# A graph layer with scattered messages: slots found earlier, shorter last segments, two banks for sums, a smaller first tile

## The chip, the cores and the metric

The kernel runs on one core of one Trainium2 chip. Its time is device microseconds of one execution; the median of three executions is given beside the time of one further execution that the hardware profiler recorded. A core has TensorE (PE, matmuls, with weight loads shown apart as PEld), VectorE (DVE), ScalarE (ACT), GpSimd (POOL) and SyncE (SP). SP, ACT and POOL can issue transfers (DMA), which share 16 DMA engines.

## The reference

One layer of message passing over 12,500 nodes of 128 features and 412,500 edges sorted by `dst`, then a residual. `ssp` is softplus minus log 2, and `idx_i` is `src`, `idx_j` is `dst`.

```python
h = jnp.maximum(_layernorm(x, axis=-1), 0.0)
h = h @ W_in2f
Wij = ssp(f_ij @ W_f1 + b_f1) @ W_f2 + b_f2
Wij = Wij * rcut_ij[:, None]
x_ij = h[idx_j] * Wij
agg = jax.ops.segment_sum(x_ij, idx_i, num_segments=h.shape[0])
out = x + ssp(agg @ W_o1 + b_o1) @ W_o2 + b_o2
```

The gather runs along the sorted index, so the rows that 512 consecutive edges gather lie close together. The sum runs along the unsorted one.

## The kernel before, in words

**Chunks and groups.** Edges go in chunks of 512 (`CH`), four tiles of 128; four chunks are a group. There are 806 chunks in 202 groups. The program is written out with no loop on the chip, and the order on each engine is the order of the calls in `step(k)`, which works on message k and on later chunks at once.

**Per chunk.** `hidden`, `hidden_log` and `hidden_end` make the softplus of the edge features, two chunks at a time (PE, three ACT passes, one DVE operation). `value` multiplies by `W_f2` into a PSUM bank and adds the bias by one matmul of `ones_b` with `bf12_p`, which holds the bias as three bf16 parts. `rows` loads a window of 32 node rows from a table in HBM (`near`), at a row that SP reads from a list; `window` and `pick` select each edge's row by a one-hot matmul; `picked` scales by the edge weight (ACT). `message` multiplies the two (L800) into a buffer `o` that holds two chunks, of which there are four. POOL then scatters each tile of 128 messages, 129 numbers each (the last is the node's place in its block of 128), by one indirect DMA into a table of slots in HBM (L804).

**Slots.** A message's slot must be free and lie in the region of its node block (98 blocks). `blocks` compares block numbers (DVE, L689), `rank` runs two matmuls over a PSUM bank `free` that carries the counts, `rank_end` takes a maximum (DVE, L713) and every group turns the result into slot numbers. This runs up to six chunks ahead of the messages (`LR`).

**Segments.** The groups are cut into segments (`SEGS`), each with its own slot table, T tiles a block (one more where a segment's own nodes lie), cleared by SP beforehand. When all messages of a segment have been scattered, `Collect` sums them: a unit is up to 6 tiles (`UT`) loaded by SP (`m`, five buffers, L842), compared with 128 places by DVE (`to`, L853), and multiplied into one PSUM bank `acc` (PE, L866) that holds a quad of four blocks. After a quad `keep` adds the bank to `agg` (DVE, L889; ACT for the first segment). Units of all segments but the last are spread over the steps by a schedule with a constant rate between the segments' ends. The last segment is collected after all chunks, in 25 quads, and each quad goes through `finish`: loads of x, matmul with `W_o1`, softplus (four ACT passes), `r` addition (L435), `x + b_o2` (DVE, L438), matmul with `W_o2`, addition (L446), store.

**Start.** `make_h` makes the node rows for a quad of four tiles (statistics, normalisation, transposes, matmul, three bf16 parts) and stores them in every table of `tables` that has them. The first table holds the first 512 rows and serves chunks 0 to 8. Two quads are made beside the first chunks, the rest from `side()`, one every nine steps. Then `bias_parts` splits the bias by eight small DVE operations.

**Fallback.** The flags in `bad` are read at the end, and `anyway` recomputes the layer if one is set. No record of it is in the profile.

Of the kernel before, what the change touches and what calls it, by code (L numbers as in the profile page):

```python
# [9 lines left out]
F32 = mybir.dt.float32  # L10
# [12 lines left out]
SEGS = (88, 40, 30, 14, 14, 8, 8)  # L23
# [6 lines left out]
UT = 6  # L30
# [11 lines left out]
def gnn_kernel(  # L42
# [38 lines left out]
    class Segment:  # L81
# [4 lines left out]
        def __init__(self, k):  # L86
# [7 lines left out]
            mean = (SEGS[k] * TG * P - (own[1] - own[0])) / QT * P / N  # L94
# [32 lines left out]


    tables = [(0, QN)]
# [4 lines left out]
    for c in range(NC):  # L134
        n = c * CH * N // n_edges
        table_of.append(0 if n < QN - NEAR - P else min(n // QN, NQ - 1) + 1)
# [46 lines left out]
    def load_x(q):  # L183
        n = min(QT, NTILE - q * QT)
        full = min(n, N // P - q * QT)
        xb = ln.tile([P, QT, P], F32, name="xb")
        if full < n:
            nc.vector.memset(xb[:, full:n, :], 0.0)
            nc.sync.dma_start(xb[:N % P, full, :], x[q * QN + full * P:N, :])
        if full:  # L190
            nc.sync.dma_start(xb[:, :full, :], x[q * QN:q * QN + full * P, :]
                              .rearrange("(c p) f -> p c f", p=P))
        return xb
# [60 lines left out]
    def constants():  # L254
# [3 lines left out]
        first_load(0)  # L258
        nc.sync.dma_start(win, w_in2f)

        for j in range(NCHUNK):
            nc.sync.dma_start(wf1[32 * j:32 * j + RBF, :], w_f1)

        nc.scalar.preload_act_table_set("natural_log_exp_and_others")
        nc.scalar.dma_start(bf1, b_f1[:, None])
        nc.scalar.dma_start(wf2, w_f2)
        nc.scalar.dma_start(bf2, b_f2[None, :].to_broadcast([P, P]))
# [4 lines left out]
        prow_i = early_room[:WP, rows_at + 5 * NC:rows_at + 5 * NC + 1].bitcast(I32)  # L272
# [7 lines left out]
        nc.gpsimd.memset(ones_b, 1.0)  # L280
        nc.gpsimd.memset(bf12_p, 0.0)
# [9 lines left out]
        nc.vector.memset(bad, 0.0)  # L291
        nc.vector.memset(rel[:, NPART - 1, :], 0.0)
        nc.vector.memset(ones, 1.0)
        nc.vector.memset(none, 0.0)

        for t in range(QT):
            nc.vector.memset(turn[:, :, t:t + 1], -1.0 if t % 2 else 1.0)
        nc.vector.tensor_scalar(prow_i, prow_i, 7, None, op0=ALU.logical_shift_right)
        nc.vector.tensor_copy(prow, prow_i)
# [3 lines left out]

    def biases(psum):

        nc.vector.tensor_scalar(nbf1, bf1, -1.0, None, op0=ALU.mult)
        b12 = psum.tile([P, QT, P], F32, name="b12", tag="acc")[:, 0, :]
        nc.tensor.matmul(b12, bf1.to_broadcast([P, P]), wf2, start=True, stop=True)
        nc.vector.tensor_add(bf12, b12, bf2)

    def bias_parts():

        left = bf12[:3, :]
        for k in range(3):
            part = ln.tile([3, P], BF16, name="bias_part", bufs=1)
            nc.vector.tensor_copy(part, left)
            nc.vector.scalar_tensor_tensor(bf12_p[:3, :], part, ident[:3, k:k + 1],
                                           bf12_p[:3, :], op0=ALU.mult, op1=ALU.add)
            if k < 2:
                nc.vector.tensor_sub(left, left, part)  # L320

    def late_loads():
        nc.sync.dma_start(wo1, w_o1)
        nc.sync.dma_start(wo2, w_o2)
        nc.sync.dma_start(bo1, b_o1[:, None])
        nc.sync.dma_start(bo2, b_o2[None, :].to_broadcast([P, P]))

    early = {}
    quads = []


    def make_h(q, psum):

        n = min(QT, NTILE - q * QT)
        xb = early.pop(q, None)
        if xb is None:
            xb = load_x(q)
# [41 lines left out]
        for (b, rows), table in zip(tables, h3_t):  # L379
            lo = max(0, b - q * QN) // P  # L380
            hi = min(n, (b + rows - q * QN) // P)
            if lo < hi:
                r = q * QN + lo * P - b
# [3 lines left out]
                if b + rows == QN:  # L387
                    yield
            if q == NQ - 1:
# [4 lines left out]
            h3[q * QN:q * QN + n * P, :].rearrange("(c p) f -> p c f", p=P),  # L394
            hb[:, :n, :, :].rearrange("p c k f -> p c (k f)"))
        yield
# [15 lines left out]
    def finish(t0, n, sT, quad, psum, tag="v", bufs=3):  # L412
# [13 lines left out]
        yield  # L426

        z = psum.tile([P, 2, CH], F32, name="z_out", tag="z")[:, 0, :n * P]
# [7 lines left out]
        for p, cs, rows in pieces:  # L436
            xi = xo[:p, cs, :]
            nc.vector.tensor_add(xi, xi, spread(bo2[:p, :], xi.shape[1]))  # L438
# [94 lines left out]
    with tc.tile_pool(name="edge", bufs=2) as edge, tc.tile_pool(  # L533
# [46 lines left out]
        class Group:  # L580


            def __init__(self, g):
# [3 lines left out]
                if g % NB == 0:  # L587
                    f = edge.tile([P, NB, CH], F32, name="f")
                    for j in range(NCHUNK):
                        nc.sync.dma_start(f[32 * j:32 * j + RBF, :, :],  # L590
                                          f_t[g:g + NB, j].rearrange("b k n -> k b n"))
                    kept["f"] = f
                self.f = kept["f"][:, g % NB, :]
                i = g - self.seg.g0
                if i % SB == 0:
                    w = min(SB, ceil_div(self.seg.c1, NCHUNK) - g) * TG
                    cols = slice(g * TG, g * TG + w)
                    src_i = edge.tile([P, SB * TG], I32, name="src_i")
                    nc.sync.dma_start(src_i[:, :w], src_t[:, cols])
                    rcut = edge.tile([P, SB * TG], F32, name="rcut")  # L600
                    nc.sync.dma_start(rcut[:, :w], rcut_t[:, cols])
                    kept["cols"] = [w, src_i, rcut]
                self.cols = kept["cols"]
                self.at = slice(i % SB * TG, (i % SB + 1) * TG)
                if g == 0:
                    rel_store(0)
                self.rel = edge.tile([WP, NCHUNK, CH], BF16, name="rel", bufs=4)
                nc.sync.dma_start(self.rel, rel_d[g * NCHUNK:(g + 1) * NCHUNK, :][None, :, :]
                                  .to_broadcast([WP, NCHUNK, CH]))
                self.inb = {}  # L610
                self.pair = {}
                self.near = {}

            def rows(self, c):

                k = self.g * NCHUNK + c
                t = table_of[k]
                i = int(k >= FIRST)
                at = k - heads[i].start
                self.near[c] = edge.tile([WP, P], BF16, name="near", bufs=8)  # L620
                start = nc.sync.value_load(shifts[i][0:1, at:at + 1], min_val=0,
                                           max_val=tables[t][1] - WR)
                nc.sync.dma_start(self.near[c], h3_t[t][bass.ds(start, WR), :]
                                  .rearrange("r (k f) -> (r k) f", f=P))

            def columns(self):
                if len(self.cols) == 3:
                    w, src_i, _ = self.cols
# [7 lines left out]
                    place = edge.tile([P, SB * TG], F32, name="place")  # L636
                    nc.vector.tensor_copy(place[:, :w], src_i[:, :w])

# [22 lines left out]
                self.rcut, self.blk, self.place, self.start = (t[:, self.at] for t in self.cols[2:])  # L661

            def hidden(self, c):

# [576 lines left out]
```

## Time and profile before

| quantity | value |
|---|---|
| median of three executions | 5252.87 us (5247.94 to 5257.49) |
| the profiled execution's own time | 4236.61 us |
| its span, first to last instruction | 4234.9 us |
| mean granted TensorE clock in it | 0.882 |
| DMA, mean over the span | 194 GB/s |
| sum matmuls, L866 | 8132 |
| compares, L853 | 824 |
| additions to `agg` by DVE, L889 | 150 |
| scatters, L804 | 3224 |

The profiled execution is 1016 us shorter than the median. Durations below are its own. A row of a group gives the line, engine, operation, tile written and read and the count; then busy time in us and the mean ns of one; then the idle time of the engine just before, and what ended it. A wait row gives who waited for what, the total in us, the times and the longest.

### The profile page before, as it was taken

How to read it: one execution, taken by the hardware profiler on the slowest of the kernel's cores; microseconds unless marked ns; L12 is line 12 of the kernel's file. 1: busy time of each engine (PE TensorE's matmuls, PEld its weight loads, DVE VectorE, ACT ScalarE, POOL GpSimd, SP SyncE). 2: the span in 40 equal slices, each digit the busy share in tenths (PEclk: the TensorE clock that was granted, in tenths of full speed). 3: DMA queues.
4: the chain of work that ended last, by engine and by line, in shares of the span. 5: the costliest groups of instructions: out<-in, count | busy, mean ns of one | idle time of the engine just before them, and what ended most of it. 6: DMA issues, size and time to landing. Idle time of an engine off the chain costs nothing. (4 is left out here: it accounts for less than half of the span.)

```text
span 4234.9 us, 73728 instructions
## 1 busy us (share of the span) xinstructions
PE 3371.9 (80%) x22378; PEld 2543.6 (60%) x22378; DVE 3352.9 (79%) x6752; ACT 2329.8 (55%) x4686; POOL 3095.9 (73%) x3246
## 2 busy tenths in 40 slices
PE   6766666666666666689998899898898988888888
PEld 4444444444444444467777777777776777767777
DVE  8877766776666656678888888888888998999978
ACT  5665565655555555555555555555555555555535
POOL 5777777777777777777777777777777777777760
PEclk9877877877777777789999999999999999999999
DMA  5765555555444454366787777877787768767667
GB/s 171 213 192 180 176 175 177 157 159 159 126 118 132 121 164 125 107 193 210 229 269 213 216 212 211 267 229 218 214 243 234 229 203 270 234 203 204 184 183 232
DMA packets 515591, 820.92 MB, mean 194 GB/s; under 512 B 177075, under 2 KB 312871, under 8 KB 515187
## 3 DMA queue, kind: packets, MB, share of 16 engines
q1 hardware_dynamic: 411586, 602.85, 49.2%
q0 software_dynamic: 103168, 213.15, 15.3%
q8 instruction: 181, 2.97, 0.3%
q14 instruction: 224, 1.83, 0.1%
q10 hardware_dynamic: 432, 0.13, 0.0%
HBM read 419.09 MB, written 396.64 MB: 193 GB/s over the span
## 5 line engine op out<-in xcount | busy, mean ns | idle before, releaser
L804 POOL DMA_INDIRECT slots<-o,slot x3224 | 3092.5, 959 | 1010.8 <-issue 770.3
L769 PE MATMUL v<-wf,r 128*128 128x128 f32 x6448 | 1066.6, 317 | 540.7 <-DVE o L800 539.1
L769 PEld LDWEIGHTS v<-wf,r 128*128 128x128 f32 x6448 | 924.7, 221 | 590.3 <-DVE o L800 571.2
L789 ACT ACTIVATE hg<-picked,rcut 128x128 f32<-128x128 f32 x3224 | 907.7, 368 | 630.9 <-PE picked L780 292.5
L866 PEld LDWEIGHTS acc<-to,m 128*128 128x128 f32 x8132 | 1017.2, 201 | 235.9 <-issue 142.0
L866 PE MATMUL acc<-to,m 128*128 128x128 f32 x8132 | 1078.8, 289 | 32.5 <-DVE to L853 22.1
L675 ACT ACTIVATE a<-z,bf 128x1024 f32<-128x1024 f32 x403 | 450.4, 1118 | 853.5 <-PE z L668 853.0
L668 PE MATMUL z<-f,wf 20*128 20x512 f32 x1612 | 527.2, 734 | 224.8 <-DVE r L684 223.3
L853 DVE TENSOR_TENSOR to<-count_ps,m 128x512 f32<-128x512 f32 (+3 forms) x824 | 641.8, 804 | 65.6 <-DMA m<-slots 34.7
L800 DVE TENSOR_TENSOR o<-v,hg 128x512 f32<-128x512 f32 x806 | 550.5, 683 | 48.8 <-PE v L771 25.0
L798 DVE COPY o<-place 128x8 f32<-128x8 f32 x403 | 77.0, 191 | 610.6 <-DMA slots<-o,slot 609.9
L760 DVE TENSOR_TENSOR at<-count_ps,rel 96x512 bf16<-96x512 f32 x806 | 545.7, 677 | 0.0
L684 DVE SCALAR_TENSOR_TENSOR r<-z,nbf,a 128x1024 f32<-128x1024 f32 x403 | 513.9, 1275 | 21.1 <-ACT a L677 21.1
L677 ACT ACTIVATE a<-a,half 128x1024 f32<-128x1024 f32 x403 | 462.8, 1148 | 13.1
L713 DVE TENSOR_REDUCE top<-free 128x4 f32<-128x392 f32 x806 | 446.7, 554 | 8.1 <-PE free L708 8.1
L689 DVE TENSOR_TENSOR inb<-count_ps,blk 128x392 f16<-128x392 f32 x806 | 447.4, 556 | 0.0
L676 ACT ACTIVATE a<-a 128x1024 f32<-128x1024 f32 x403 | 426.0, 1057 | 12.8
L780 PEld LDWEIGHTS <-at 96*128 96x128 bf16 x3224 | 256.0, 105 | 251.1 <-DVE at L760 104.0
L668 PEld LDWEIGHTS z<-f,wf 20*128 20x128 f32 x1612 | 138.8, 210 | 409.6 <-DVE r L684 362.2
L780 PE MATMUL picked<-near,at 96*128 96x128 bf16 x3224 | 343.2, 234 | 32.1 <-DVE at L760 26.8
L771 PE MATMUL v<-bf_p,ones_b 128*128 128x512 bf16 x806 | 353.3, 438 | 0.0
L741 PE MATMUL free<-inb,rest_of 128*128 128x392 f16 x806 | 302.9, 376 | 12.6 <-DVE top L713 12.6
(112 smaller groups left out, 1428.2 us busy)
## 6 DMA issues: line engine op xcount, KB each, us to landing
m<-slots SPq DMA_DIRECT2D x311, 387.0 KB
m<-slots SPq DMA_DIRECT2D x317, 258.0 KB
rel<-rel_d SPq DMA_DIRECT2D x202, 384.0 KB
m<-slots SPq DMA_DIRECT2D x172, 322.5 KB
slots<-o,slot POOLq DMA_INDIRECT x3224
slots<-zero SPq DMA_DIRECT2D x96, 387.0 KB
slots<-zero SPq DMA_DIRECT2D x64, 516.0 KB
f<-in_f_t SPq DMA_DIRECT2D x404, 80.0 KB
```

The source lines that it names most:

```text
L668: nc.tensor.matmul(z[:, k, :], wf1[rows, :], self.f[rows, :], start=True, stop=True)
L675: nc.scalar.activation(a, z, AF.Abs, bias=bf1)
L677: nc.scalar.activation(a, a, AF.Ln, bias=half, scale=0.5)
L684: nc.vector.scalar_tensor_tensor(r, z, nbf1, a, op0=ALU.max, op1=ALU.add)
L760: nc.vector.tensor_tensor(at, prow_ps.to_broadcast([WP, CH]), self.rel[:, c, :], op=ALU.is_equal)
L769: nc.tensor.matmul(v[:, i, :], r[:, i * P:(i + 1) * P], wf2, start=i == 0, stop=False, skip_group_check=True)
L780: nc.tensor.matmul(ps[:, i, :], at[:, i * P:(i + 1) * P], near, start=True, stop=True)
L789: nc.scalar.activation(hg[:, i, :], ps[:, i, :], AF.Copy, scale=self.rcut[:, j:j + 1])
L800: nc.vector.tensor_mul(o[:, :, :P], v, hg)
L804: put = nc.gpsimd.indirect_dma_start(out=views[j % VIEWS], out_offset=bass.IndirectOffsetOnAxis(ap=self.slot[:, j:j + 1], axis=0), in_=o[: ...
L853: nc.vector.tensor_tensor(to[:, :n, :], count_ps[:, None, :].to_broadcast([P, n, P]), self.m[u][:, :n, P:].to_broadcast([P, n, P]), op=ALU ...
L866: nc.tensor.matmul(self.acc[b // QT][:, i, :], m[:, j, :P], to[:, j, :], start=t == 0, stop=t == self.seg.tiles(b) - 1)
```

## The change

- `LEAD`, `ahead`: slots are found six chunks ahead up to chunk 100, then one more every four chunks, up to 64. What ranking needs moves out of `Group` into a class `Places` with its own `columns`; slot numbers and places get more buffers. Up to step 20 (`RAMP`) the lead grows by 1.25 chunks a step.
- `SEGS` has nine segments that end with 3, 3 and 4 groups, where the size formula gives one tile a block. `UT` is 4, `m` has nine buffers, `to` takes buffers of the node stage.
- `sums_tile`: once the last chunk is ranked, every second quad sums in the bank that held `free`. The sum matmuls of a unit follow its compare at a distance that `add` sets, and banks are emptied at three places in a step.
- The schedule counts 3.3 tiles for each end of a quad, and its steps are worth 1.3 from chunk 742 on.
- `finish`: POOL adds b_o2 to x as soon as x is there; the z matmuls of the last quads alternate between two halves of one tile.
- Start: the first node tile alone (`made_h`), with a table of its own that serves chunks 0 to 4; the bias parts come from copies on ACT and subtractions on DVE beside the first tile; loads and constants are reordered.

```diff
-SEGS = (88, 40, 30, 14, 14, 8, 8)
+SEGS = (88, 41, 25, 18, 12, 8, 3, 3, 4)
+LEAD = 64
-UT = 6
+UT = 4
...
-            mean = (SEGS[k] * TG * P - (own[1] - own[0])) / QT * P / N
+            edges = min(n_edges, self.c1 * CH) - self.c0 * CH
+            mean = (edges - (own[1] - own[0])) / QT * P / N
...
+    made_h = [(0, 1), (1, QT - 1)]
+    made_h += [(t, min(QT, NTILE - t)) for t in range(QT, NTILE, QT)]
-    tables = [(0, QN)]
+    tables = [(0, P), (0, QN)]
...
-        table_of.append(0 if n < QN - NEAR - P else min(n // QN, NQ - 1) + 1)
+        table_of.append(0 if n <= P - 2 * WR else 1 if n < QN - P - WR
+                        else min(n // QN, NQ - 1) + 2)
...
+        for p, cs, rows in pieces:
+            xi = xo[:p, cs, :]
+            nc.gpsimd.tensor_add(xi, xi, spread(bo2[:p, :], xi.shape[1]))
...
-        for p, cs, rows in pieces:
-            xi = xo[:p, cs, :]
-            nc.vector.tensor_add(xi, xi, spread(bo2[:p, :], xi.shape[1]))
...
+        def sums_tile():
+            kept["banks"] = kept.get("banks", 0) + (made["rank"] == NCH - 1 and not ranked)
+            if kept["banks"] % 2:
+                return state_ps.tile([P, QT, P], F32, name="acc_b", tag="free")
+            return psum.tile([P, QT, P], F32, name="acc")
...
-                m = edge.tile([P, UT, RW], F32, name="m", bufs=5)
+                m = edge.tile([P, UT, RW], F32, name="m", bufs=9)
...
-                        self.acc[b // QT] = psum.tile([P, QT, P], F32, name="acc")
+                        self.acc[b // QT] = sums_tile()
...
+        RAMP = 20
+        LEAD_AT = 100
+        LATE = NCH - LEAD
...
+        def ahead(k):
+            lead = LR if k < LEAD_AT else min(LR + (k - LEAD_AT) // 4, LEAD)
+            return min(k + lead, k + 1 + (k + 1) * (LR - 1) // RAMP, NCH - 1)
...
+        def pace(k):
+            return k + 0.3 * max(0, k - LATE)
+        def cost(c, u):
+            return c.units[u][1] * c.units[u][3] + 3.3 * c.ends(u)
...
-            for c, u in units:
-                c.load(u + AHEAD)
+            def add(most):
+                while len(summed) > most:
+                    c, u = summed.pop(0)
+                    c.add(u)
+            def waiting():
+                return late and summed and summed[0][0].seg.T == 1
...
+            if waiting():
+                add(1)
+            for seg, u in units:
+                seg.load(u + AHEAD)
...
-            summed[0].add(summed[1])
-            summed[0].keep()
+            for c, u in summed:
+                c.add(u)
+                c.keep()
...
+            zs = psum.tile([P, 2, CH], F32, name="z_out", tag="z")
-                outs.append(finish(b, n, sT, quad, psum, *tag))
+                outs.append(finish(b, n, sT, quad, psum, *tag, z=zs[:, b // QT % 2, :]))
```

## The prediction

> **What bounds the kernel now.** I read the page's engine and group tables first, then windows of 150 us, the waits of single stretches, and the timeline at both ends.
>
> ```profile
> PE 3371.9 (80%) x22378; PEld 2543.6 (60%) x22378; DVE 3352.9 (79%) x6752; ACT 2329.8 (55%) x4686; POOL 3095.9 (73%) x3246
> ...
> L804 POOL DMA_INDIRECT slots<-o,slot x3224 | 3092.5, 959 | 1010.8 <-issue 770.3
> ```
>
> Three windows (busy us and count of PE, weight loads, VectorE, ScalarE, POOL; then granted clock, DMA share, GB/s):
>
> ```profile
> 1650.00:1800.00 150.00, 100.86 (x517) 63.44 (x514) 95.53 (x202) 82.00 (x165) 113.81 (x119) 0.78 0.40 111
> ...
> 3300.00:3450.00 150.00, 139.27 (x1077) 114.85 (x1076) 142.32 (x255) 87.15 (x176) 113.71 (x120) 0.98 0.77 226
> ...
> 4140.00:4200.00 60.00, 58.76 (x406) 48.86 (x406) 58.02 (x94) 39.01 (x63) 0.00 (x0) 1.00 0.87 260
> ```
>
> No engine looks full on average, yet POOL holds the pace. A scatter takes 959 ns and the next starts 0.30 us later, for no wait that the profile shows: 119 or 120 in every window, whether VectorE is at 95 or at 142 of 150 us. The timeline starts them 1.264 us apart, so a chunk of four costs 5.055 us. The waits agree: VectorE waits for the scatters to free `o`, mostly before sums are collected (398.0 us in 600 to 1800, 94.6 in 1800 to 2600), hardly later.
>
> ```profile
> DVE o L798 <- DMA slots<-o,slot: 609.9, 191, 7.8
> ...
> SPq L842 <- PE acc L866: 861.6, 355, 12.1
> ```
>
> So VectorE's lead is a store of time. Counted in the timeline, chunk 600's message ends at 3042.4 and its first scatter starts at 3067.0 (24.6 us); the lead is 15.1 at chunk 740 and 8.6 at chunk 800. The collecting stretch is balanced on an edge.
>
> ```profile
> 26.11 1.13 POOL L804 DMA_INDIRECT slots<-o,slot  x1 [21.83 <-DVE o L800]
> ...
> 73.09 0.96 POOL L804 DMA_INDIRECT slots<-o,slot  x1 [0.31 <-DVE inb L689]
> ...
> 4106.56 0.96 POOL L804 DMA_INDIRECT slots<-o,slot  x1 [0.30 <-issue]
> ...
> 4124.27 1.86 DVE L853 TENSOR_TENSOR to<-count_ps,m 128x512 f32<-128x512 f32 x3
> ...
> 4226.66 1.07 DVE L446 TENSOR_TENSOR xo<-xo,v_out 128x512 f32<-128x512 f32 x3
> ```
>
> The span therefore splits: 26.1 to the first scatter; 6.6 lost before chunk 8 (73.09-26.11-8x5.055); an unbroken run to 4107.5; 16.8 until the last segment's first compare; 93.1 for its 25 quads of blocks; 17.5 of drain. Only the ends can give time while POOL keeps its pace.
>
> **What the Trainium skill says.** "GPSIMD Engine Reference", section 3.1, prices an addition of two fp32 tensors of 2048 columns at 4497 ns on GpSimd, 156 of it dispatch; my estimate for 512 columns is 156+4341/4 = 1.24 us. No such addition is in this trace. "SBUF — State Buffer", section "Who interferes with whom", says that a VectorE instruction with two SBUF inputs and a GpSimd one that reads SBUF exclude each other; no run here shows it yet. "Perfetto Trace Analysis", section "DMA Instruction — SWDGE (GPSIMD)", says that the recorded span ends with descriptor writing, not with the move; the trace agrees, since VectorE waits for buffers long after the 959 ns.
>
> **The change, part by part.**
>
> *First node tile alone.* On the first scatter's chain it removes three of four statistics pairs (1.2 us), three normalisations (0.84), three transposes (0.6), six of eight matmul passes (1.0), and narrows three ScalarE copies from 0.60 to about 0.28 (1.0 together) and two subtractions from 0.68 to about 0.28 (0.8). The bias parts, eight small VectorE operations between 20.3 and 22.6, no longer sit ahead of the bias matmul (up to 2). Sum 7.4; SP's queue gains issues of about 0.45 us each ahead of the relative rows, so I take -7 (bounds 0 to -10). The stall goes next to chunk 5: the 128-row table serves chunks 0 to 4, then three more tiles must be stored and landed. Slower ranking (1.25 instead of 1.5 chunks a step, 1.25 us each) pays for that: ramp loss unchanged, 0 (-4 to +6).
>
> *Slots 64 ahead.* A chunk's rank is VectorE 0.556 (blocks) + 0.554 (maximum) + 0.14 (a quarter of three small ones) = 1.25 us, and two PE passes of 0.375. It is only moved: 58 chunks, 72 us of VectorE and 43 of PE, leave the last 64 steps for chunks 100 to 332, +0.3 us a step where VectorE idles over 1 us a step. Worth nothing there.
>
> *Segments and pieces of at most 4 tiles.* From the segment formula: 775 units and 3860 tiles before the last segment become 1175 and 4074; the last goes from 49 units, 206 tiles to 27 and 108. A compare costs 133 ns a tile plus 148 (548 ns for 3, 681 for 4, 946 for 6). In the loop: 400x0.148+214x0.133 = 88 us; two more segments add 50 additions of 0.686 = 34, read-outs 7, four batches of columns 15. Of 144 us busy about 105 remain, as back-to-back VectorE instructions overlap by some 75 ns (compares 1.28 for two). Less the 72 moved: +33 us net in about 2300, and PE +214x2x0.13-43 = +13. POOL hides it: slack is the 94.6 us of waits plus the lead. It is uneven: chunks 776 to 800 carry about 5.75 us of PE a step, 17 us over POOL's pace; the lead, rebuilt in chunks 742 to 776 where no ranks are left, should cover it. Charge +3 (0 to +15); with the cover gone +33. SP issues 400 more loads of about 0.4 us, 160 in 2300, and nine buffers instead of five shorten its waits (861.6 on `acc`); queued behind them are the window rows, loaded twelve chunks ahead. Nothing.
>
> *Two banks for sums.* From 4095 to 4124 a quad takes 2.83 us: PE 2.05, then 0.78 until VectorE has emptied the only bank. The second bank exists once all ranks are done. A one-tile quad then costs VectorE 0.64+0.61 = 1.25 us against 1.0 of PE. About 14 quads remain after the last chunk, 17 us, much as the 10 at 2.83 before. The last segment starts some 12 us after POOL ends instead of 16.8: -5 (-12 to +4).
>
> *The last segment's 25 quads.* 3.75 us each now: PE 2.0 (sixteen sum matmuls)+0.54+1.21 = 3.75, VectorE six operations of about 0.62. After: PE 1.0+0.54+1.21 = 2.75; VectorE 2.5 (one compare and the x+b_o2 addition gone), ScalarE 2.5, POOL 1.24 for its addition, which can hold up VectorE's r addition by up to that. DMA decides: it is at 0.87 in this stretch. Its packets there average 27.9 ns at 512 bytes and 53.5 at 1032; a quad is 1024 of the first (x, out) and 512 of the second, 3.5 us on 16 engines. Packets of 516 bytes have no row; at half the longer price to the shorter one a quad would be 2.65 to 2.7, at the same 0.9 efficiency 3.0. I take 3.0 (2.7 to 3.5): 25x0.75 = -19 (-26 to -6). Drain unchanged.
>
> Sum: -7+0+3-5-19 = -28 us against the profiled execution's own 4236.6 us (span 4234.9): 4208.6. The median is 1016 us above that execution, and nothing in the profile says where. If it is POOL's (0.315 us more a scatter), ends and savings stay as they are, and the body gains slack. I carry -28 over: 5252.9-28 = 5225.
>
> **Rivals.** (1) *The scatters starve.* VectorE and PE in 1800 to 4100 exceed POOL's pace. For it: 142.3 of 150 busy, the lead falling to 8.6. Against: 72 us are taken out of exactly the tightest steps. Each 0.15 us a step above POOL's pace over 445 steps is 67 us; minus a 25 us lead that is +42, less the 31 gained at the ends: from there it is slower, to 5260 to 5300. (2) *The tail is held by DMA.* If 516-byte packets cost nearly what 1032-byte ones do (40 ns and over), a quad stays at 3.2 to 3.5; with a start that gains little, 5243. (3) *The unexplained 1016 us falls on work that the change adds* (1.35 us for each of 775 units, say) rather than on POOL: 400 units more would cost far more than the ends give, to 5350 or over. (4) *The change does less than it says*: the second bank comes only at chunk 742, and the quads already collected by then stay at one bank; that is in the sum.
>
> **From cases to numbers.** Forecast 0.62 (own range 5190 to 5242); tail held by DMA 0.15; starving 0.16; the added work carrying the hidden time 0.07. A measurement of this kernel tells about 0.2%, 10.5 us. The forecast and half of the second case are faster, 0.70; the rest of the second and a starving that just cancels the ends, 0.12; slower, 0.18. Range 5185 to 5275: both ends of the tail and the start below, starving above.
>
> **What would show it.** First scatter near 19 us and chunk 8's near 66; 119 to 120 scatters in every window to the last; the last one near 4100; last compares single per quad, quads 3.0 us apart; no VectorE addition of `bo`, 26 on POOL of about 1.2 us. Wrong: POOL waiting for `o` after chunk 600, or quads still above 3.5 us.

## The result and the profile after

The changed kernel takes 5298.5 us (median of four executions, 5283.3 to 5318.2) against 5251.1 us of the kernel before beside it (5247.9 to 5257.5). The ratio is 1.008, 95% interval 1.0056 to 1.0103: slower by 0.8%. The forecast of 5225 us and its range up to 5275 were wrong, and so was the sign.

All executions of a set of runs go one of two ways, whatever the kernel and even on one chip, and the kernel before then takes either about 4250 us or 5251 to 5343 us (medians of the sets); the profiled execution that the prediction worked from (4236.6 us) was of the first kind, the timings were of the second, and so is the profile after (a span of 5281.6 us). Below, the first kind is called *prompt* and the second *late*, for a reason that the waits show. A ratio always compares kernels within one set of runs; a trace is of one execution.

The page of the changed kernel, engines and the costliest group. A row of a group ends with the idle time of the engine before it and who ended most of it:

```profile
PE 3822.6 (72%) x22610; PEld 2847.9 (54%) x22610; DVE 3440.7 (65%) x7236; ACT 2334.4 (44%) x4695; POOL 3171.5 (60%) x3276
...
L847 POOL DMA_INDIRECT slots<-o,slot x3224 | 3134.7, 972 | 2013.2 <-DVE o L843 1128.1
```

Before, POOL was idle for 1010.8 us in front of its scatters, most of it (770.3 us) for no wait that the profile shows. Now it is idle for 2013.2 us, 1128.1 of it waiting for VectorE's message. A scatter takes 972 ns instead of 959. The windows, with the columns of those shown of before:

```profile
1650.00:1800.00 150.00, 91.62 (x426) 59.05 (x427) 83.62 (x175) 67.78 (x134) 94.13 (x97) 0.67 0.39 117
3300.00:3450.00 150.00, 121.02 (x801) 96.84 (x800) 104.15 (x213) 66.64 (x135) 89.82 (x93) 0.87 0.58 174
...
5195.00:5255.00 60.00, 50.01 (x304) 37.70 (x304) 46.28 (x66) 41.51 (x67) 21.10 (x16) 0.99 0.73 205
```

POOL makes 97 and 93 scatters in 150 us where it made 119 and 120, and no engine is full instead: VectorE is busy for 84 and 104 of 150 us. The waits of the changed kernel say who waits for whom ("remote" is a releaser that the profile can't name):

```profile
POOL slots L847 <- DVE o L843: 1128.1, 409, 15.5
...
DVE o L843 <- remote: 774.0, 169, 9.6
...
ACT hg L832 <- remote: 466.4, 99, 9.1
```

The timeline of the changed kernel in another late execution (e11 below) shows what such a wait is. For one message PE makes `picked` (L823), then `v` and its bias (L812, L814); ScalarE scales `picked` (L832), and VectorE multiplies (L843):

```profile
1002.54 0.40 PE L823 MATMUL picked<-near,at 96*128 96x128 bf16 x4
...
1004.53 0.63 PE L814 MATMUL v<-bf_p,ones_b 128*128 128x512 bf16 x1
...
1005.95 1.12 ACT L832 ACTIVATE hg<-picked,rcut 128x128 f32<-128x128 f32 x4
...
1010.72 0.69 DVE L843 TENSOR_TENSOR o<-v,hg 128x512 f32<-128x512 f32 x1 [6.21 <-remote]
...
1011.47 0.71 PEld L812 LDWEIGHTS v<-wf,r 128*128 128x128 f32 x3 [5.48 <-DVE o L843]
```

PE is done with both operands by 1005.2 and ScalarE by 1007.1, but VectorE starts at 1010.72, and PE, which wants the bank back, then starts again too. The trace records no signal of PE's between 1002 and 1010.6 and then three within 0.1 us, over 4 us after the last end of a PE instruction (1006.25).

Between the end of a PE instruction and the semaphore that it raises lie 14 ns (median) in a prompt execution and 267 ns in the profile after, with a quarter over 1.7 us and the latest of them coming together in bursts. ScalarE's and VectorE's recorded semaphores are as prompt there as ever (9 and 11 ns). Two things weaken these figures: the ends of PE's instructions are modelled, and late traces lack records (the profile after has 80% of PE's semaphore updates and about half of ScalarE's and VectorE's, e20 has 99% of each).

The starts of the instructions say the same without those records. From the moment when `v`, `hg` and VectorE itself are free to the start of the multiply, chunks 20 to 799 lose 1019 us in all in e8 (the kernel before late, but for one small addition) and nothing in e0 (the kernel before prompt). That is nearly the whole 1055 us between their spans. VectorE still follows ScalarE within 0.03 us (median, `r` after `a`), and POOL starts a message's first scatter within 0.31 us of VectorE's multiply and its own last scatter, late as prompt. Nor are the transfers slower: a packet of 516 bytes takes 32 ns late (e11) and 33 prompt (e20), and VectorE waits for only 0.4 us in all for scatters to free `o` (609.9 before).

So in late executions the pace is not POOL's: it is that of the chain PE to ScalarE and VectorE and back, in which every hand-off from PE (the next engine's wait for its signal) can be late. VectorE's lead over POOL is then 0.3 to 2.6 us at nearly every chunk, against 24.6 at chunk 600 before. What makes the signals late is not known. The mean granted clock is lower in late executions (0.805 after, 0.882 before), SyncE's own register operations are drawn out too (411 us in e11, 192 in e20), and records are missing; each may be cause or consequence.

The ends, from POOL's and VectorE's timeline of the changed kernel:

```profile
20.67 1.13 POOL L847 DMA_INDIRECT slots<-o,slot  x1 [15.54 <-DVE o L843]
...
5152.05 0.97 POOL L847 DMA_INDIRECT slots<-o,slot  x1 [0.30 <-issue]
...
5179.81 1.27 DVE L906 TENSOR_TENSOR to<-count_ps,m 128x512 f32<-128x512 f32 x2
...
5274.71 0.48 DVE L460 TENSOR_TENSOR xo<-xo,v_out 128x128 f32<-128x128 f32 x2 [0.17 <-PE v_out L456]
```

The first scatter comes 5.4 us sooner than before. After the last scatter there are 26.8 us to the last segment's first compare.

### The profile page after: what moved, and what is told of

It is laid out like the page before. It is cut to its first block, busy times and chain, and to the rows that moved or that the text cites. A ratio compares the mean times of both kernels' runs of the same rounds, so it can differ in the third digit from the quotient of the medians.

```text
span 5281.6 us, 75647 instructions
## 1 busy us (share of the span) xinstructions
PE 3822.6 (72%) x22610; PEld 2847.9 (54%) x22610; DVE 3440.7 (65%) x7236; ACT 2334.4 (44%) x4695; POOL 3171.5 (60%) x3276
## 4 chain that ended last, share of the span: by engine, by line
## 5 line engine op out<-in xcount | busy, mean ns | idle before, releaser
L847 POOL DMA_INDIRECT slots<-o,slot x3224 | 3134.7, 972 | 2013.2 <-DVE o L843 1128.1
L832 ACT ACTIVATE hg<-picked,rcut 128x128 f32<-128x128 f32 x3224 | 906.2, 369 | 1444.8 <-remote 466.4
L812 PE MATMUL v<-wf,r 128*128 128x128 f32 x6448 | 1184.7, 341 | 478.0 <-DVE o L843 432.2
L843 DVE TENSOR_TENSOR o<-v,hg 128x512 f32<-128x512 f32 x806 | 552.5, 686 | 1350.2 <-remote 774.0
L812 PEld LDWEIGHTS v<-wf,r 128*128 128x128 f32 x6448 | 1035.3, 244 | 531.9 <-DVE o L843 464.0
L919 PE MATMUL acc<-to,m 128*128 128x128 f32 x7484 | 1133.9, 305 | 217.8 <-issue 161.3
L919 PEld LDWEIGHTS acc<-to,m 128*128 128x128 f32 x7484 | 1043.0, 215 | 452.5 <-issue 364.8
L781 PE MATMUL z<-f,wf 20*128 20x512 f32 x1612 | 561.5, 771 | 178.9 <-DVE r L797 92.7
L906 DVE TENSOR_TENSOR to<-count_ps,m 128x512 f32<-128x512 f32 (+2 forms) x1202 | 673.4, 608 | 17.9 <-DMA m<-slots 17.9
L823 PEld LDWEIGHTS <-at 96*128 96x128 bf16 x3224 | 279.2, 112 | 337.7 <-issue 213.7
L823 PE MATMUL picked<-near,at 96*128 96x128 bf16 x3224 | 377.8, 247 | 83.3 <-issue 45.2
L682 PEld LDWEIGHTS <-after 128*128 128x128 f16 x806 | 92.5, 115 | 579.5 <-issue 529.7
L814 PE MATMUL v<-bf_p,ones_b 128*128 128x512 bf16 x806 | 378.0, 469 | 0.3 <-issue 0.3
```

The source lines that it names most:

```text
L781: nc.tensor.matmul(z[:, k, :], wf1[rows, :], self.f[rows, :], start=True, stop=True)
L812: nc.tensor.matmul(v[:, i, :], r[:, i * P:(i + 1) * P], wf2, start=i == 0, stop=False, skip_group_check=True)
L823: nc.tensor.matmul(ps[:, i, :], at[:, i * P:(i + 1) * P], near, start=True, stop=True)
L832: nc.scalar.activation(hg[:, i, :], ps[:, i, :], AF.Copy, scale=self.rcut[:, j:j + 1])
L843: nc.vector.tensor_mul(o[:, :, :P], v, hg)
L847: put = nc.gpsimd.indirect_dma_start(out=views[j % VIEWS], out_offset=bass.IndirectOffsetOnAxis(ap=places_of[self.g].slot[:, j:j + 1], axi ...
```

## The experiments

The question for each: does it act on POOL's pace or on the hand-offs? Letters in the recorded expectations name theories; most are explained where they stand. A says that late hand-offs, not POOL, set the pace; F that GpSimd's addition lengthens every scatter; H and I concern the start; J that the moved ranks and the added short segments cost the chain of hand-offs; K that the number of units does.

### First set: prompt

> The kernel before, unchanged, for a trace taken beside the changed kernel's. Theory A (PE's signals come late in these executions, in both kernels; in the changed kernel's trace a quarter of them come over 1.7 us after the modelled end of the matmul): 5251 us within 6, and a trace with 97 to 101 scatters per 150 us already before any sums are collected, not 119. Theory B (the changed kernel alone is slowed, by VectorE and PE in the collecting stretch): the trace shows 119 scatters per 150 us throughout and a span near 4235.

> The changed kernel with slots found only 6 chunks ahead; the schedule of units is kept, so the last 64 steps carry the ranks again, and the second bank comes only for the last six chunks. Theory A (hand-offs of PE are what a step pays for, and moving ranks removes none): 5270 to 5320, within 0.5% of the changed kernel, with the loss at the end about equal to the gain in chunks 100 to 332. Theory C (the long lead is what made it slower, since ranks are added to steps that have no slack in chunks 100 to 332, 58 of about 0.6 us): 5240 to 5260.

> The changed kernel with pieces of up to 6 tiles as before and six buffers for them, so 824 units or a few more instead of 1202. Theory A (each unit is one more hand-off from SP's load over VectorE's compare to PE and back): at least half of the 47 us comes back, 5250 to 5275. Theory D (the size of pieces is hidden and the loss is from the order in the step, the lead or the segments): within 0.3% of the changed kernel, 5283 to 5315.

> The changed kernel with the seven segments of before (88, 40, 30, 14, 14, 8, 8). Theory A: 50 fewer quads to add and 60 to 80 fewer units, against a last segment of two tiles a block (about 25 us more at the end): 5290 to 5320. Theory E (the short segments, with their clears, read-outs and column batches, are the loss): 5255 to 5275 in spite of the longer end.

```diff
# e1: changed kernel, slots found six chunks ahead
-LEAD = 64
+LEAD = 6
-        LATE = NCH - LEAD
+        LATE = NCH - 64
# e2: changed kernel, units of up to six tiles
-UT = 4
+UT = 6
-                m = edge.tile([P, UT, RW], F32, name="m", bufs=9)
+                m = edge.tile([P, UT, RW], F32, name="m", bufs=6)
# e3: changed kernel, the old segments
-SEGS = (88, 41, 25, 18, 12, 8, 3, 3, 4)
+SEGS = (88, 40, 30, 14, 14, 8, 8)
```

| kernel | median, us | ratio to before (4251.4) | 95% |
|---|---|---|---|
| e0, before again | 4255.4 | 1.0003 | 0.9995 to 1.0011 |
| e1, lead of 6 | 4388.2 | 1.0316 | 1.0299 to 1.0333 |
| e2, units of 6 tiles | 4272.0 | 1.0044 | 1.0030 to 1.0059 |
| e3, old segments | 4267.1 | 1.0034 | 1.0023 to 1.0046 |

The times expected for these four were those of late executions, and the set came out prompt. So e0 could not tell A from B; e8 below can, and has 97 to 99 scatters in 150 us before any sums, as A has it.

Neither the small units nor the short segments explain a loss here: with either undone the kernel stays 0.3 to 0.4% slower. The lead of 64 matters, though. With 6, chunks 740 to 805 take 448 us against 334 in the changed kernel (e20 below): VectorE is busy for 359.8 of them, and POOL waits 131.2 us for its messages. Three things act in e1 at once: the 58 ranks are back in these steps (72 us of VectorE), the second bank comes only for the last six chunks (VectorE waits 67.6 us there for the one bank), and the schedule still packs more sums into these steps. The prediction's argument against starving, that "72 us are taken out of exactly the tightest steps", is borne out in its direction, but e1 does not part the three.

### GpSimd's addition and the scatters

A scatter took 972 ns instead of 959, for all 3224, although the last of them starts at 5152.1 us and the first addition at 5172.0. Four runs say what does it, in late sets; the ratio of e4, e5 and e6 is to 5342.6 us, that of e8 to 5328.1.

> The changed kernel, unchanged, beside the kernel before at 4251. Theory F (each scatter takes some 12 ns longer on POOL in every kernel built from the changed one: 968 to 972 in the traces so far against 959 to 961): 3224 times 12 ns is 39 us, the start loses 8 more by chunk 20, the end gives back 20 to 25, so 4262 to 4285, with a mean scatter of 970 to 973 ns. Theory G (scatters cost the same and the ends give what was forecast): 4220 to 4235. If PE's signals are late in this execution too: near 5298.

> The changed kernel with x + b_o2 back on VectorE, after the r addition. Theory F1 (a GpSimd addition anywhere in the program makes POOL handle each scatter slower): the mean scatter falls to 958 to 962 ns and the time by 30 to 40 us, less 5 to 15 that VectorE's extra 0.68 us a quad costs at the end. Theory F2 (the length of a scatter comes from something else, such as where the lists and buffers lie in SBUF): 970 to 973 ns, and 0 to 15 us slower than the changed kernel.

> The kernel before with x + b_o2 by GpSimd ahead of the z matmul, that part of the change alone. F1: mean scatter 968 to 973 ns and 4280 to 4292. F2: 958 to 962 ns; VectorE loses one of six operations of a quad at the end, but PE holds a quad at 3.75, so 4245 to 4255.

> The kernel before with one GpSimd addition of a single column at the very start, and nothing else changed. Theory F1 (that the program holds such an addition is enough to make every scatter longer): mean scatter 967 to 970 ns instead of 960. Theory F3 (it takes additions near the scatters): 958 to 962 ns. In time: where PE's signals are on time and POOL sets the pace (kernel before near 4251), F1 gives 4272 to 4282; where they are late (before near 5250 to 5340), POOL is not the bound and F1 gives no difference, within 0.3%.

```diff
# e5: changed kernel, x + b_o2 on VectorE again (e6 does the reverse to the kernel before)
-            nc.gpsimd.tensor_add(xi, xi, spread(bo2[:p, :], xi.shape[1]))
+            nc.vector.tensor_add(xi, xi, spread(bo2[:p, :], xi.shape[1]))
# e8: kernel before, one addition of a single column among the constants
+        nc.gpsimd.tensor_add(zero[:, 0:1], zero[:, 0:1], zero[:, 1:2])
```

The scatter groups of e5, e6 and e8, in this order:

```profile
L846 POOL DMA_INDIRECT slots<-o,slot x3224 | 3096.2, 960 | 2154.8 <-DVE o L842 1261.9
```

```profile
L804 POOL DMA_INDIRECT slots<-o,slot x3224 | 3122.7, 969 | 2057.2 <-DVE o L800 1172.0
```

```profile
L805 POOL DMA_INDIRECT slots<-o,slot x3224 | 3122.0, 968 | 2045.9 <-DVE o L801 1152.7
```

In all traces of this case a scatter takes 959 to 963 ns (mean) without a GpSimd addition and 968 to 972 with one, and one addition of one column at the very start does the same as 26 at the end, 24 of them of 512 columns. So it is not contention: that an addition of GpSimd's is in the program at all adds 6 to 12 ns to each scatter, compared within a set. How it does so is not shown, nor whether another kind of instruction would do the same. In time no loss shows here (e6 and e8 are even 0.2% faster than before): e4 5385.0 (ratio 1.0083, 1.0052 to 1.0113), e5 5390.6 (1.0084, 1.0061 to 1.0107), e6 5329.4 (0.998, 0.9964 to 0.9996), e8 5320.3 (0.9983, 0.9969 to 0.9997). POOL waits over 1150 us for messages in these sets and can spare 3224 times 9 ns. What it costs in a prompt set is settled by the last two runs.

### Start, lead and schedule, late

> The changed kernel with RAMP 10 in place of 20: slots are found 1.5 chunks a step again and the steady order begins at step 10. Theory H (the slower ranking and the unsteady order up to step 20 lose what the earlier first scatter gains): the first scatter of chunk 20 moves from 140 to 143 us to 130 to 135, and the time falls by 6 to 10. Theory I (the early chunks wait for the second table, not for ranks): chunk 20 stays within 2 us and so does the time.

> The changed kernel with LEAD 6, and with it all that follows from it: the schedule takes only the last six chunks for light steps, and the second bank comes there. Theory J (with late signals a step costs its chain of hand-offs through PE, so a rank added to a step costs about 0.2 us and packing sums into the last 64 steps costs more than it saves): with late signals chunks 100 to 360 take 10 to 14 us less than in the changed kernel, and chunks 740 to 805 20 to 40 us less, so 15 to 50 us faster in all. Theory K (the loss comes with the number of units, not with the lead): within 10 us of the changed kernel. With signals on time I expect 20 to 60 us slower than the changed kernel, as VectorE is short of time in the last chunks.

> The changed kernel with a pace that does not rise: units spread evenly over the steps instead of more of them in the last 64. Theory J: with late signals chunks 780 to 805 take 15 to 30 us less and the chunks before 740 5 to 15 more, 5 to 20 us faster in all. Theory K: within 5 us. With signals on time: chunks 740 to 805 have slack, the chunks before it starve POOL, 5 to 30 us slower.

> The changed kernel unchanged, as the measure for the other runs of this call. With signals on time (kernel before near 4251): scatters of 969 ns cost 28 us against 960, the start 8, and the end gives 15 to 25, so 4255 to 4270. With late signals: 0.6 to 1.0% slower than the kernel before.

```diff
# e7
-        RAMP = 20
+        RAMP = 10
# e9
-LEAD = 64
+LEAD = 6
# e10
-            return k + 0.3 * max(0, k - LATE)
+            return k
```

e7 took 5377.2 us (ratio to 5342.6: 1.0058, 1.0034 to 1.0082) and started chunk 20 at 157.7 us, as the others do: theory H missed. e9 took 5385.0 (1.0108, 1.0064 to 1.0151), e10 5385.1 (1.0101, 1.0062 to 1.0140), e11, the change itself, 5365.2 (1.0082, 1.0058 to 1.0106), these three to 5328.1 us. A flat schedule (e10) is another miss, with 196 us for chunks 780 to 805 against 188. The lead takes and gives: e9 has 1596 us for chunks 100 to 360, where e11 builds its lead of 58 ranks and takes 1608, but its end after the last scatter is 164 us long instead of 125. The 20 to 40 us that J expected of e9 in chunks 740 to 805 do not appear (460 us against 462).

### What loses the time, late

By now e11 against e8 (the kernel before but for one small addition, same chip) showed where: of 45.5 us, 15.9 in chunks 100 to 360, 2.6 to chunk 640, 24.2 in 640 to 740 and 18.1 in the rest, with -14.5 after the last scatter. Units, short segments, or both?

> The kernel before with units of up to 4 tiles instead of 6 (UT 4, seven buffers for m); segments, lead, banks, start and end as before. It has some 400 units more and the same tiles. Theory K (it is the number of units, each with its own compare and its own hand-off between PE and VectorE): where the kernel before takes 5250 to 5340 us it is 20 to 50 us slower than before, nearly all of it in chunks 360 to 805; where the kernel before takes about 4250 us, 10 to 30 us slower. Theory J (it is the extra quads of the two added segments and the moved ranks): within 10 us of the kernel before in either case.

> The changed kernel with units of up to 6 tiles (UT 6, six buffers for m), all else as changed. Theory K: where the kernel before takes 5250 to 5340 us, chunks 640 to 805 lose under 15 us instead of 42, and the whole is 15 to 40 us faster than the changed kernel there, so within 20 us of the kernel before, perhaps faster. Theory J: no more than 10 us faster than the changed kernel's +42. Where the kernel before takes about 4250 us: 4272 again.

> The changed kernel with the seven segments of the kernel before, units still of up to 4 tiles. Theory J (extra quads, and short segments whose work is packed into few steps): where the kernel before takes 5250 to 5340 us, chunks 640 to 805 lose under 15 us, but the end gives nothing, so some 10 to 25 us over the kernel before. Theory K: chunks 640 to 805 still lose 25 us or more. Where the kernel before takes about 4250 us: 4267 again.

> The changed kernel with units of up to 6 tiles, the seven old segments, and x + b_o2 back on VectorE: what is left of the change is the lead of 64, the second bank, the start, the schedule's new costs and the order in a step. If the longer scatters cost 28 us where the kernel before takes about 4250 us, and the small units and short segments cost the rest, it is 5 to 20 us faster than before there. Where the kernel before takes 5250 to 5340 us, the scatters' length does not count; theories K and J together expect -10 to +10, and a loss of 15 us in chunks 100 to 360 from the lead remains inside it.

```diff
# e12: kernel before
-UT = 6
+UT = 4
-                m = edge.tile([P, UT, RW], F32, name="m", bufs=5)
+                m = edge.tile([P, UT, RW], F32, name="m", bufs=7)
# e13 is e2, e14 is e3; e15 is e2, e3 and e5 together
```

| kernel | median, us | ratio to before (5262.7) | 95% |
|---|---|---|---|
| e12, before with units of 4 | 5334.3 | 1.0136 | 1.0097 to 1.0174 |
| e13, change with units of 6 | 5266.3 | 1.0009 | 0.9993 to 1.0026 |
| e14, change with old segments | 5237.5 | 0.9956 | 0.9945 to 0.9967 |
| e15, both, and VectorE's addition | 5226.5 | 0.9945 | 0.9918 to 0.9972 |

Beside e4's ratio of 1.0083 (of another set), taking the short segments out turns +0.8% into -0.4%, some 67 us. Taking the small units out as well gives 0.1% more, which the intervals of e14 and e15 do not tell from nothing, though by itself (e13) it gives 0.7%. Theory J holds for the segments, and by more than it foretold: e14 and e15 are 25 and 36 us faster than before. K holds only where something else is short. In e12 the waits point to the buffers `to`: there are three of them, released by PE's late signals. VectorE's waits in e12, and then in e8, which has units of six:

```profile
DVE to L853 <- PE acc L866: 312.0, 178, 4.9
DVE to L853 <- remote: 189.7, 53, 5.1
```

```profile
DVE to L854 <- PE acc L867: 120.0, 59, 5.4
DVE to L854 <- remote: 66.1, 19, 5.5
```

That is 502 us instead of 186 before compares. The changed kernel has six such buffers (three tags of a pool of two) and shows no wait for them (its one wait at L906, 17.9 us, is for loads). No run gave e12 more of them, so this part is argued.

The stage that carries most of the segments' cost is chunks 780 to 805. The profile after and e14 reach chunk 640 within 4 us of each other (4014.4 and 4018.6), so they can be laid side by side. Chunks 780 to 805 of the changed kernel late, of e14 late, and of the changed kernel prompt (e20 below); columns as before:

```profile
4955.90:5148.20 192.30, 143.57 (x974) 124.73 (x973) 121.66 (x202) 63.40 (x129) 96.93 (x100) 0.85 0.55 152
```

```profile
4931.50:5090.80 159.30, 129.42 (x810) 107.72 (x810) 93.07 (x153) 63.39 (x129) 96.88 (x100) 0.81 0.54 154
```

```profile
4033.40:4160.70 127.30, 110.75 (x879) 97.58 (x877) 113.34 (x191) 50.71 (x103) 96.88 (x100) 0.99 0.79 216
```

In these 25 chunks the changed kernel empties 51 banks into `agg`, e14 24. VectorE's busy time and its waits fill the late stages: 121.7 + 70.6 = 192.3 and 93.1 + 66.1 = 159.2. The waits are about equal, so most of the 33 us is VectorE's own added work, 28.6 us, and it lies on the path. Within one set it is the same: e13, with the short segments, takes 189.0 us here and VectorE is busy for 122.2; e15, without them, takes 161.9 and 92.2. Prompt, VectorE has nearly as much to do (113.3 us) but waits 13.8 us in all, and POOL's 100 scatters set the 127.3 us: the same work is hidden. All of the changed kernel's VectorE waits in this stage, late, are for banks of sums; the two largest rows:

```profile
DVE agg L942 <- remote: 24.1, 7, 6.3
DVE agg L942 <- PE acc L919: 16.5, 8, 4.8
```

### The last two: the change itself prompt, and a version that is faster both ways

> The changed kernel as it is, beside the version below. Where the kernel before takes about 4250 us: 4270 to 4295, since its two variants with one part undone took 4267 and 4272 there, and the scatters lengthened by GpSimd's additions alone are 28 us of it. Where the kernel before takes 5250 to 5340 us: ratio 1.006 to 1.011 again, with 185 to 192 us in chunks 780 to 805.

> The changed kernel with units of up to 6 tiles, the seven old segments, and x + b_o2 on VectorE, on the same chip as the run above. Where the kernel before takes about 4250 us: scatters of 958 ns again, and 5 to 20 us faster than before. If the longer scatters are not what costs there, it is 4265 or more like the others. Where the kernel before takes 5250 to 5340 us: ratio 0.991 to 0.998 again, with about 160 us in chunks 780 to 805; a ratio of 1 or over would say that the runs before were not comparable.

e20 took 4266.9 us (ratio to 4248.4: 1.0035, 1.0023 to 1.0048) and e21, the kernel of e15, 4236.8 (0.9966, 0.9954 to 0.9979); the first is 3 us under what was expected, the second within it. The change as it stands is slower both ways, for different reasons. The version without its small units, short segments and GpSimd addition is 0.3% faster prompt and 0.55% faster late.

The scatter rows of e0, e20 and e21:

```profile
L804 POOL DMA_INDIRECT slots<-o,slot x3224 | 3098.8, 961 | 1020.2 <-issue 772.8
```

```profile
L847 POOL DMA_INDIRECT slots<-o,slot x3224 | 3131.4, 971 | 1029.0 <-issue 754.8
```

```profile
L846 POOL DMA_INDIRECT slots<-o,slot x3224 | 3094.1, 960 | 1020.5 <-issue 776.9
```

Here POOL does set the pace, and the 10 ns count. (e0 is of another chip than e20 and e21; the kernel before took 4251.4 and 4248.4 us beside them.) Chunks 100 to 700, with a lead of 12 to 27 us at both ends, take 3036.0 us in e0, 3060.3 in e20 and 3034.6 in e21; the difference of e20 is 2400 scatters of 10 ns. e1, e2 and e3, which undo the lead, the small units or the short segments and keep the addition, take 3058.9, 3059.4 and 3053.7 us there. So in these chunks it is the addition. No prompt run takes it out alone, and of the 30 us between e20 and e21 as a whole these chunks show 26.

The difference of the spans by stage, each difference after minus before, us, one execution each:

| stage | prompt, e20 - e0 | late, e11 - e8 |
|---|---|---|
| to the first scatter | -5.4 | -5.3 |
| from there to chunk 20 | +15.7 | +3.8 |
| chunks 20 to 100 | +3.3 | +0.7 |
| 100 to 360 | +11.0 | +15.9 |
| 360 to 700 | +13.3 | +17.1 |
| 700 to the last scatter | +4.4 | +27.8 |
| after the last scatter | -24.8 | -14.5 |
| span | +17.5 | +45.5 |

## Why the prediction was wrong

**The carry-over failed first.** "If it is POOL's (0.315 us more a scatter), ends and savings stay as they are, and the body gains slack": the missing 1016 us are not POOL's but PE's late signals. Late, POOL has the slack, VectorE and PE have none, and work that POOL's pace had hidden comes onto the path. Rival 3, that the unexplained time falls on added work, was the right kind and had 0.07. Its size, 1.35 us for each unit, was not (400 units would be 540 us, far beyond the 5350 that it named): small units cost 0.7% beside the short segments and about 0.1% without them (e13, e14, e15). It is rather what VectorE has to do in the fullest steps. The profile and the median were of two different balances, and a sum made against one said little of the other. Prompt, where nothing had to be carried over, the sum fails too: +17.5 us between the spans instead of -28, mainly by the scatters' duration and the ramp (below).

**Rival 1, starving,** named 5260 to 5300 us, and the time fell just there, by luck; its sign, POOL waiting for `o` after chunk 600, is in the profile after as well (1128.1 us in the whole execution). But late, POOL waits so in the kernel before too (1152.7 us in e8), from the first chunks on. What the change adds to it sits in chunks 100 to 360 and from 640 on, so the rival had the place of the second part, and not the reason: prompt, with the lead that the prediction relied on, the change starves POOL for only 10 us.

**"Only the ends can give time while POOL keeps its pace"** is right prompt (POOL's scatters fill chunks 780 to 805 of e20) and not late.

**The scatters' own duration was left out of the sum.** The addition was priced at 1.24 us on GpSimd and any cost was sought in its collisions; that its presence lengthens all 3224 scatters was on no side of the bound. Prompt it is +24.3 us in chunks 100 to 700 alone, as much as the whole end gives.

**First node tile, -7 and a ramp of 0 (-4 to +6).** The first scatter came 5.4 us sooner, inside the bounds. The ramp's term was mis-sized: +15.7 us to chunk 20, prompt. The stall did go to chunk 5, as written, but what was to pay for it did not. POOL's timeline in e20, chunks 4, 5, 6 and 8:

```profile
48.67 0.97 POOL L847 DMA_INDIRECT slots<-o,slot  x1 [2.21 <-DVE o L843]
...
60.03 0.97 POOL L847 DMA_INDIRECT slots<-o,slot  x1 [6.58 <-DVE o L843]
...
66.05 0.97 POOL L847 DMA_INDIRECT slots<-o,slot  x1 [1.23 <-DVE o L843]
...
80.10 0.97 POOL L847 DMA_INDIRECT slots<-o,slot  x1 [3.31 <-DVE o L843]
```

Then the waits between 20 and 145 us, of e0 and of e20:

```profile
PE picked L780 <- DMA near<-h: 5.2, 1, 5.2
...
DVE top L713 <- PE free L708: 7.6, 5, 2.5
```

```profile
PE picked L823 <- DMA near<-h: 8.1, 1, 8.1
...
DVE top L687 <- PE free L682: 30.2, 14, 6.9
```

The wait for the second table's rows costs 6.6 us, and after it most chunks lose over a microsecond more; in this stretch VectorE waits for the rank matmuls 14 times instead of 5. That these waits are the reason is not shown: a shorter ramp was tried late only (e7), where chunk 20 comes as soon as before either way.

**Slots 64 ahead, worth nothing; body +3 (0 to +15), +33 without cover.** Prompt, the body without the scatters' share is about level. The lead rebuilt as foreseen, from 1.6 us at chunk 740 to 24.2 at chunk 780; around 740 POOL starved for about 10 us, which the kernel before, starved later (0.8 us of lead at 780), does not. Late, the cover is gone and it costs +45 from chunk 360 to the last scatter and +16 in the 260 chunks before, where ranks are brought forward. That is the case for which the prediction had +33, near in size, and which it took for unlikely.

**Two banks, -5; 25 quads at 3.0 us, -19.** Prompt the end gives 24.8 us against 24 foreseen, but by other shares, so the sum is right by luck. From POOL's end to the last segment's first compare it is 8.2 us in e20 instead of 20.1 in e0 (16.8 in the profile before): 12 us, not 5, for the bank, the moved ranks and the schedule together. From quad to quad (additions to `agg`) it is 3.53 us instead of 3.93, not 3.0: 2.9 up to the thirteenth quad, where e0 has 3.7, and 4.2 from there, as in e0. The second half, in e20:

```profile
4198.29 1.65 DVE L452 TENSOR_TENSOR r_out<-r_out,a_out 128x512 f32<-128x512 f32 x1
4201.03 0.69 DVE L906 TENSOR_TENSOR to<-count_ps,m 128x512 f32<-128x512 f32 x1 [1.10 <-DMA m<-slots]
...
4205.00 0.69 DVE L906 TENSOR_TENSOR to<-count_ps,m 128x512 f32<-128x512 f32 x1 [1.48 <-DMA m<-slots]
```

VectorE waits for loads. SyncE issues them in order behind a load of x, and that one waits for a store to free one of six `xo` buffers (the queue's wait between 4195 and 4262):

```profile
SPq L437 <- DMA out<-xo: 40.0, 17, 3.7
```

The kernel before has this wait too (24.5 us in the second half of e0), and its quads are as slow there; more buffers were not tried. That is rival 2's result, but not its mechanism: a packet of 516 bytes takes 31 ns in this stretch, not 40, and between 4200 and 4240 the DMA engines are busy for 0.72 of the time, less than the 0.87 from which its price came. Late, the end gives 14.5: to the last segment's first compare it is 25.0 us in e11 and 26.7 in e8, so the bank gives little there.

**GpSimd's addition, 1.24 us.** An undisturbed one of 512 columns takes 1.26 to 1.28 us, and up to 1.80 beside VectorE's work (e20). The Trainium skill's "GPSIMD Engine Reference", section 3.1, gives the 4497 ns for 2048 columns from which the estimate came. The 156 ns in the estimate stand there for VectorE's dispatch, and GpSimd's has no figure, so that 1.24 comes so close is partly luck. The collision with VectorE's `r` addition is there: 1.65 us at 4198.29 instead of 0.68, beside an addition of GpSimd's from 4198.12 to 4199.39, as "SBUF — State Buffer", section "Who interferes with whom", has it. Not every addition meets one, and e5 shows no gain from its absence late.

## What to carry to other kernels

When the profiled execution and the median differ by a fifth, first find which engine's signals or durations differ, and price the change in both balances: what one engine's pace hides in one is on the path in the other. More banks to empty and more pieces to compare are VectorE's own time wherever hand-offs are slow; packing them into the last steps makes those steps the bound. Check the duration of the pacing instruction itself after any change to its engine's program: prompt, 10 ns on each of 3224 scatters cost all that the end had won.

## What the runs showed of the hardware

- PE's completion signals can come late for whole executions (median 267 ns after the modelled end, a quarter over 1.7 us, in bursts), while VectorE follows ScalarE within 0.03 us as ever. The kernel before then takes 5251 to 5343 us instead of about 4250. One and the same chip was prompt in the first set (e0) and late in the next (e4); the cause stays open. Traces of such executions lack about half of the semaphore updates of ScalarE and VectorE.
- One elementwise addition by GpSimd in the program, even of one column at the start, makes every indirect scatter 6 to 12 ns longer (medians 958 to 962 ns without, 967 to 971 with).
- Packets of 516 bytes took 31 ns in the last stretch of e20, those of 512 bytes 28 and those of 1032 bytes 55 (means).
